# Turning the node coordinates of a two-layer graph network on VectorE and through DRAM instead of on TensorE, with the last pair's first graph handled early

## The chip, the core and the metric

The kernel runs on one core of a Trainium2 chip. The metric is device time in microseconds (us) of one execution, as a median of several. The core has five engines that each take their own instructions in written order: TensorE (PE in the profile, with its weight loads as PEld), VectorE (DVE), ScalarE (ACT), GpSimd (POOL) and SyncE (SP), which here issues nearly all DMAs. Matmul results land in PSUM, which has eight banks; everything else on the chip lies in SBUF, whose first dimension is the partition.

## The reference

There are 64 graphs of 256 nodes with 256 features, with a dense 0/1 adjacency each, all in float32. Layer 0 has a convolution branch (a 1x1 and a 17-tap convolution over nodes, both with batch norm), a message branch and a gated unit. Layer 1 is a graph convolution between two layer norms. Cut to what matters:

```python
s = x @ w_se.T + b_se                              # 3 coordinates for each node
sq = jnp.sum(s * s, axis=-1)
dist = sq[:, :, None] + sq[:, None, :] - 2.0 * jnp.einsum('bnd,bmd->bnm', s, s)
A = jnp.exp(-dist) * mask                          # mask is the adjacency
msg = jax.nn.relu(x @ w_msg.T + b_msg)
x_nmp = jnp.einsum('bnm,bmd->bnd', A, msg)
x_in = jnp.concatenate([x_conv, x_nmp], axis=-1)   # gates r, z, n from x_in and x
x = _layernorm(x + (1.0 - z) * nn_ + z * x)
...
h = layer_norm(x, ln_gamma, ln_beta)
agg = jnp.einsum('bij,bjh->bih', adj, h)
conv = jnp.einsum('bkh,ho->bko', agg, W_rel) + b_rel + jnp.einsum('bkh,ho->bko', h, W_root)
x = _layernorm(x + x + jax.nn.relu(conv))
```

The change touches the way that s gets from "nodes on partitions" to "coordinates on partitions", and the order of layer 1 for the last two graphs.

## The kernel before, in words

Graphs go in 32 pairs (function `pair(p)`), and the convolution goes in 8 batches of 8 graphs (`conv1`, `conv`); the first batch has its own setting-up of the filters. A pair takes these steps. Its x, turned so that features lie on partitions, is loaded (xT, L1077), and its adjacency (adjm, L1080). PE multiplies it by the message weights and, in three more columns, by the coordinate weights (ps_msg, L1095); DVE adds the bias (L1102).

**The coordinates.** ACT copies the three coordinates of each node into sts (L1104), POOL works out the squared lengths (L1109 to L1113) and puts -sq/2 beside them (L1112). PE turns this with two transposes (ps_sT, L1119). ACT copies the result twice into lr (L1120, with one row set to one by means of the small table `lone`, and L1121). Eight matmuls of four rows each (in the trace; four in the code) then give s.s - sq/2 for each pair of nodes (ps_dist, L1128). Each graph and node half has its own four partitions of lr, at 0, 32, 64 and 96. ACT takes the exponential (AT, L1132), DVE multiplies by the adjacency (L1135), and PE multiplies with the messages (ps_nmp, L1142).

**The gates.** 126 matmuls per pair (L1194), by a scheme of seven products in place of eight, or 144 by the plain way (L1180) in the first two pairs and the last. ACT and DVE make r, z, n and the sum x + layer 0 out of them: wT (L1285; in the last pair `turn_in`, L1218 to L1227, does it for one feature half of one graph at a time).

**Layer 1.** `norm` turns wT to nodes on partitions. Most pairs do that with one VectorE transpose in 32x32 blocks (L1302), four stores to DRAM (wd, L1306) and four loads (x1, L1310); the last pair does it with PE transposes (ps_wT, L1324). Statistics follow, with a power on POOL (L1344). `project` multiplies by both weight matrices (ps_hy, L1359), and DVE scales and adds on the way out (L1361). `aggregate` multiplies by the adjacency (ps_agg, L1373); then come DVE (L1376, L1377), the second norm and the store of the output (L1403). For the last pair (`apart`), norm and project run for graph 0 and then for graph 1; then aggregation for graph 0, and `last_nodes` (L1405), which aggregates, norms and stores graph 1 in two halves of its nodes. There is one copy of wT, x1 and HY, so pair p + 1 writes them when pair p has read them.

**The order of the work.** Nothing runs as it stands in the code. Each operation carries a key (`prog.at(key, step)`), most of them relative to `due = FIRST_GATES + p * PERIOD`. A planner (`scheduled`, L319) then walks through time: on each engine it takes, of the operations that are ready in its own estimate, the one with the smallest key, less a lead for DVE operations and for those that empty a PSUM bank. Its estimates of durations stand at L288 to L311. A load on SP is not planned before its key. The order that comes out is each engine's written program; at run time an instruction waits for its semaphores, and all behind it on its engine wait too. Operations in `prog.group()` stay together. `hold` and `need` add dependences: an instruction with `hold=[v]` goes after all earlier readers of v.

Of the kernel before, what the change touches and what calls it, by code (L numbers as in the profile page):

```python
# [14 lines left out]
F32 = mybir.dt.float32  # L15
# [3 lines left out]
P = 128  # L19
B, N, D = 64, 256, 256  # L20
C = D // P
# [33 lines left out]
OB = 7  # L55
HQ = 2 * M * C * (M + 1)
XC_SLOTS = BG + 2
FIRST_GATES, PERIOD, GATE_TIME = 124.4, 57.9, 16.7
AHEAD_FROM, AHEAD_TO, W_DEEP = -57.8, -17.6, 2
CONV1_FROM, CONV1_TO, CONV_FROM, CONV_OUT, CONV_TO = -10.0, 196.6, -12.4, -57.1, -31.9  # L60
PAIR_LEAD, FILTER_LEAD, LOAD_AHEAD = 31.8, 15.0, 22.3
SMALL_RUNS, TURN_FROM = 1.3, 2
KEEP = 7.7
LATE_LAG = 17.7
W_FROM, W_LAG = 2, 20.1
PLAIN, SUMS_FROM = (0, 1, B // 2 - 1), 2


# [190 lines left out]
def dram_cells(ap):  # L259

    name = ap.tensor.name
    if not name.startswith(("w2m", "xt", "hd", "wd")):
        return []
    dims = list(ap.ap)
    top = ap.offset + sum(s * (n - 1) for s, n in dims)
    return [(name, u) for u in range(ap.offset // DRAM_UNIT, top // DRAM_UNIT + 1)]


class Engine:
# [4 lines left out]
    def __getattr__(self, method):  # L274
        program, name = self.program, self.name

        def call(*args, hold=(), need=(), lines_up=0, **named):
            line = sys._getframe(1 + lines_up).f_lineno
            outs = [v for v in (named.get("out"), named.get("accum_out"), named.get("out_")) if v is not None]
            outs += [] if "out" in named else [args[0]]  # L280
            ins = [v for v in list(args) + list(named.values()) if not any(v is o for o in outs)]
            if method == "matmul" and not named.get("start", True):
                ins.append(outs[0])

            def places(vs):
                return [v if isinstance(v, View) else dram_cells(v) for v in vs
                        if isinstance(v, View) or hasattr(v, "tensor")]
            n = max((v.size() for v in outs if isinstance(v, View)), default=0)  # L288
            moved = 0
            if method == "dma_start":  # L290
                v = outs[0] if isinstance(outs[0], View) else named["in_"]
                dur, moved = 0.06, v.size() * v.at.shape[0] * 4
                if not isinstance(outs[0], View) and outs[0].tensor.name.startswith("w2m"):
                    moved *= 0.65
                if program.joined is not None:
                    moved *= SMALL_RUNS
            elif name == "tensor":
# [120 lines left out]
def gnn_two_layers(  # L418
# [65 lines left out]
    h_dram = tc.dram_tile([B // 2, 5, P, D], F32, name="hd")  # L484
    xt_dram = tc.dram_tile([B // 2, P, C, 2 * N], F32, name="xt")
    w_dram = tc.dram_tile([2, SQ, 2 * C * C, P // SQ, P], F32, name="wd")
    W2 = sb("w2all", [P, C, NM, D], "first")
    taps = sb("taps", [TAPS * OB, NM * OB], "filters")

# [455 lines left out]
    bms = sb("bms", [P, D + 4])  # L945
    wrr = sb("wrr", [P, C, 2 * D])
    hrow = sb("hrow", [P, 2 * D])
    lone = sb("lone", [LR, 2])
    gb = sb("gb", [P, 2, C])
    bih = sb("bih", [P, 3, C])  # L950
    bhh = sb("bhh", [P, 3, C])
    half_r = sb("half_r", [P, C])
    half_z = sb("half_z", [P, C])
    sts = sb("sts", [P, LR + P + 4])
    sts.base.fine = 0
    lr = sb("lr", [P, 2, N])
    prog.at(22.0, 0.001)
    ab = np.zeros((LR, 2), np.float32)
    for r in range(0, LR, SR):
        ab[r:r + 3, 0] = 1.0  # L960
        ab[r + 3, 1] = 1.0
    SP.dma_start(out=lone, in_=nc.inline_tensor(ab, name="last_row_one").ap())
    G.memset(sts, 0.0)
    V.memset(wms[:, :, D + 3:], 0.0)
    SP.dma_start(out=wms[:, :, :D], in_=wmsgT.rearrange("(c p) n -> p c n", p=P))
    SP.dma_start(out=wms[:, :, D:D + 3], in_=wseT.rearrange("(c p) n -> p c n", p=P))
# [105 lines left out]
    def pair(p):  # L1072
# [7 lines left out]
            SP.dma_start(out=adjm[:, g], in_=adjT[2 * p + g].rearrange("(c p) n -> p c n", p=P))  # L1080

        prog.at(due - 62, 0.6)
        at = p % 2 * 4
        st = sts[:, at:at + C * LR].rearrange("p (m e) -> p m e", m=C)

        def places(m):
            o = at + m * LR
            return sts[:, o:o + 4 * SR].rearrange("p (g r e) -> p g r e", g=2, r=2)[:, :, :, 0:3]
        idle = p < 2
        for g in range(2):  # L1090
            for m in range(C):
# [9 lines left out]
                    continue  # L1101
                V.tensor_add(msg[:, g, m], ps[:, :D + 4], bms)  # L1102
        for m in range(C):
            A.copy(places(m), msg[:, :, m, D:D + 3].unsqueeze(2).to_broadcast([P, 2, 2, 3]))  # L1104
        for g in range(2):
            A.activation(msg[:, g, :, :D], msg[:, g, :, :D], AF.Relu)
        sq, ns = next(sqs), next(nss)
        s = st[:, :, :3 * SR].rearrange("p m (r e) -> p m r e", e=SR)[:, :, ::2, 0:3]
# [3 lines left out]
        G.tensor_scalar(st[:, :, 3::SR].rearrange("p m (g r) -> p m g r", g=2), ns.unsqueeze(3).to_broadcast([P, C, 2, 2]), -0.5, None, ALU.mult)  # L1112
        G.tensor_scalar(ns, ns, -1.0, None, ALU.mult)  # L1113

        prog.at(due - 45, 0.3)
        ps = bank("ps_sT")
        with prog.group():
            for m in range(C):
                PE.transpose(ps[:LR, m * P:(m + 1) * P], st[:, m, :LR], ident, hold=[lr])  # L1119
        A.activation(lr[:LR, 0, :], ps[:LR, :N], AF.Identity, bias=lone[:, 1:2], scale=lone[:, 0:1])  # L1120
        A.copy(lr[:LR, 1, :], ps[:LR, :N])  # L1121
        prog.at(due - 38, 0.3)
        pss = [bank("ps_dist") for _ in range(2 * C)]
        with prog.group():
# [167 lines left out]
            return [(g, m, 2 * g + m) for g in gs for m in range(C)]  # L1292

        def norm(gs):
            prog.at(due + 2 * GATE_TIME + (4 if 0 in gs else -10), 0.3)
            q, sh = next(qs), next(shs)
            js = slice(2 * gs[0], 2 * gs[-1] + 2)
            total, squares, mv = next(totals), next(totals), next(mvs)
# [18 lines left out]
                        A.activation(HY[:, g, m, :D], x1[:, g, m, :], AF.Copy, accum_out=total[:, j:j + 1])  # L1317
            for g in gs if apart or p < W_FROM else ():
                ps = bank("ps_wT")
                with prog.group():  # L1320
                    for m in range(C):
                        for f in range(C):
                            at = m * D + f * P
                            PE.transpose(ps[:, at:at + P], wT[:, 2 * f + g, m * P:(m + 1) * P], ident,  # L1324
                                         hold=[x1[:, g]])
# [25 lines left out]
            return q  # L1351

        def project(gs, q):
            prog.at(due + 2 * GATE_TIME + (8 if 0 in gs else -6) + (0.0 if apart or p < W_FROM else LATE_LAG if late else W_LAG), 0.6)
            for g, m, j in spots(gs):
                ps = bank("ps_hy")
                with prog.group():
                    for f in range(C):
                        PE.matmul(ps, wT[:, 2 * f + g, m * P:(m + 1) * P], wrr[:, f, :], start=(f == 0),  # L1359
                                  stop=(f == C - 1), hold=[HY[:, g, m]], need=[] if apart else [q[:, 1, j:j + 1]])  # L1360
# [189 lines left out]
```

## Time and profile before

| what | value |
|---|---|
| median of 3 runs (lowest, highest) | 2005.71 us (2005.5, 2005.9) |
| the profiled execution: time, span | 2005.27 us, 2003.5 us |
| mean granted TensorE clock | 0.999 |
| PE busy | 1989.3 us, 99% |
| DVE, ACT, POOL busy | 1716.0, 1031.9, 286.2 us |
| DMA queue q1, share of 16 engines' span | 48.2% |
| ps_sT, 64 matmuls | 12.3 us busy |
| ps_dist, 256 matmuls | 22.8 us busy |

The span runs from the first instruction of the program to the end of the last. Busy time counts an engine's own work; matmuls are pipelined, so that the busy time of one group holds parts that overlap with its neighbours. The chain of waits goes back from the last instruction to what released each step, and so says which engine the end was waiting for at each moment.

### The profile page before, as it was taken

The page shows a single profiled execution, that of the slowest core. Times are in us where ns is not written, and L with a number is a line of the kernel's source. Part 1 is how long each engine was busy: PE and PEld are TensorE (multiplying, and loading weights), DVE is VectorE, ACT ScalarE, POOL GpSimd, SP SyncE. Part 2 cuts the span into 40 slices and gives each one's busy share as a digit, 9 for nine tenths or more (in the row PEclk, how much of TensorE's full clock was granted, in tenths as well). Part 3 has the DMA queues.
Part 4 walks back from the last instruction along what each step waited for, and adds up shares of the span by engine and source line. Part 5 has one row for each costly group of instructions (what it writes and reads, how often), then busy time and mean ns, then how long its engine had stood idle before and what let it go on. Part 6 is the DMA issues. An engine that isn't in the chain of part 4 may idle for free.

```text
span 2003.5 us, 28397 instructions
## 1 busy us (share of the span) xinstructions
PE 1989.3 (99%) x10068; PEld 1615.5 (81%) x10068; DVE 1716.0 (86%) x2632; ACT 1031.9 (52%) x2410; POOL 286.2 (14%) x521
## 2 busy tenths in 40 slices
PE   9999999999999999999999999999999999999997
PEld 6787888778888888778887788878888888887785
DVE  7787899999989998999979999899998999876755
ACT  7535433754456454655357545375535644556442
POOL 4200210111110111111011111011111111211001
PEclk9999999999999999999999999999999999999999
DMA  8844355535645456535645357453575245422311
GB/s 219 294 139 146 100 181 148 150 85 167 177 128 150 121 149 169 142 94 141 186 143 149 77 144 200 127 149 93 152 191 152 78 115 143 116 59 78 86 46 40
DMA packets 449114, 271.60 MB, mean 136 GB/s; under 512 B 247253, under 2 KB 433612, under 8 KB 448972
## 3 DMA queue, kind: packets, MB, share of 16 engines
q1 hardware_dynamic: 448430, 269.36, 48.2%
q8 instruction: 79, 1.29, 0.3%
q14 instruction: 63, 0.52, 0.1%
q10 hardware_dynamic: 542, 0.43, 0.1%
HBM read 193.05 MB, written 76.68 MB: 135 GB/s over the span
## 4 chain that ended last, share of the span: by engine, by line
PE 97%; DVE 1%; ACT 1%; POOL 0%; DMA 0%; issue 0%; POOLq 0%; ACTq 0%; DVEq 0%
PE ps_a L1194 22%; PE ps_k L716 17%; PE ps_d L1194 11%; PE ps_hy L1359 11%; PE ps_msg L1095 6%; PE ps_c L847 6%; PE ps_agg L1373 5%; PE ps_b L1194 5%; PE ps_nmp L1142 5%; PE ps_g L1180 4%; PE ps_w L574 2%; PE ps_dist L1128 1%; PE ps_tT L557 0%; PE ps_sT L1119 0%; PE ps_xTc L826 0%; PE ps_msg L1098 0%
## 5 line engine op out<-in xcount | busy, mean ns | idle before, releaser
L716 PEld LDWEIGHTS ps_k<-XF,cs 128*128 128x128 f32 x2632 | 312.6, 192 | 13.5 <-issue 7.0
L716 PE MATMUL ps_k<-XF,cs 128*128 128x128 f32 x2632 | 314.6, 275 | 0.0
L1359 PE MATMUL ps_hy<-wrr,wT 128*128 128x512 f32 x512 | 225.4, 592 | 0.0
L1194 PE MATMUL ps_a<-nmp,WB 128*128 128x256 f32 x696 | 207.1, 379 | 0.3 <-ACT nmp L1144 0.3
L1208 ACT ACTIVATE RG<-ps_a,bhh 128x512 f32<-128x512 f32 x116 | 79.4, 684 | 225.5 <-PE ps_a L1194 189.6
L1359 PEld LDWEIGHTS ps_hy<-wrr,wT 128*128 128x128 f32 x512 | 96.3, 190 | 107.7 <-issue 103.2
L1194 PE MATMUL ps_a<-tx,WB 128*128 128x256 f32 x522 | 155.7, 382 | 0.9 <-ACT RG L1208 0.9
L1194 PEld LDWEIGHTS ps_a<-nmp,WB 128*128 128x128 f32 x696 | 132.1, 190 | 18.7 <-ACT nmp L1144 0.7
L1095 PE MATMUL ps_msg<-wms,xT 128*128 128x260 f32 x512 | 133.2, 383 | 0.0
L688 DVE TENSOR_TENSOR XF<-XF 128x512 f32<-128x512 f32 (+3 forms) x128 | 126.8, 1007 | 4.9 <-ACT XF L769 3.1
L1142 PE MATMUL ps_nmp<-AT,msg 128*128 128x256 f32 x512 | 118.5, 379 | 0.0
L1361 DVE SCALAR_TENSOR_TENSOR HY<-ps_hy,q,hrow 128x512 f32<-128x512 f32 x128 | 95.2, 746 | 27.0 <-PE ps_hy L1359 21.9
L1373 PE MATMUL ps_agg<-HY,adja 128*128 128x256 f32 x504 | 117.6, 379 | 0.0
L1194 PEld LDWEIGHTS ps_a<-tx,WB 128*128 128x128 f32 x522 | 96.1, 190 | 23.0 <-issue 9.2
L1373 PEld LDWEIGHTS ps_agg<-HY,adja 128*128 128x128 f32 x504 | 94.7, 190 | 22.5 <-issue 9.3
L1383 ACT ACTIVATE HY<-HY 128x256 f32<-128x256 f32 x112 | 46.1, 415 | 129.5 <-DVE HY L1377 129.5
L1206 ACT COPY ZN<-ps_a 128x512 f32<-128x512 f32 x116 | 67.5, 582 | 84.7 <-PE ps_a L1194 84.7
L1095 PEld LDWEIGHTS ps_msg<-wms,xT 128*128 128x128 f32 x512 | 94.6, 190 | 18.7 <-issue 7.2
L851 ACT ACTIVATE xn<-ps_c,bnsh,bnsc 128x256 f32<-128x256 f32 x112 | 58.5, 564 | 98.5 <-PE ps_c L847 94.6
L847 PE MATMUL ps_c<-xTc,w 128*128 128x512 f32 x232 | 108.5, 594 | 0.0
L1142 PEld LDWEIGHTS ps_nmp<-AT,msg 128*128 128x128 f32 x512 | 96.1, 190 | 12.4
L1194 PE MATMUL ps_d<-nmp,WB 128*128 128x256 f32 x348 | 103.6, 379 | 1.3 <-DVE nmp L1163 1.3
(224 smaller groups left out, 4413.1 us busy)
## 6 DMA issues: line engine op xcount, KB each, us to landing
cs<-w2m SPq DMA_DIRECT2D x105, 768.0 KB, 5.0
adjm<-in_adjT_dram SPq DMA_DIRECT2D x64, 256.0 KB, 3.4
xT<-xt SPq DMA_DIRECT2D x32, 512.0 KB, 3.7
adja<-in_adjT_dram SPq DMA_DIRECT2D x64, 256.0 KB, 2.8
out_dram<-HY SPq DMA_DIRECT2D x63, 256.0 KB, 2.2
hd<-xn SPq DMA_DIRECT2D x28, 544.0 KB, 3.0
XF<-hd SPq DMA_DIRECT2D x28, 544.0 KB, 4.0
xt<-xTc SPq DMA_DIRECT2D x29, 512.0 KB, 3.6
```

What stands on the lines that cost most here:

```text
L688: (V.tensor_add if add else V.tensor_sub)(sl(o, n), sl(a, n), sl(b, n))
L716: PE.matmul(ps[:, o * P:(o + 1) * P], w(m, c)[:, o * P:(o + 1) * P], X[:, slot, c * P:(c + 1) * P], start=first and o == 0 and c == 0, sto ...
L847: PE.matmul(ps, w1[:, c, o * P:(o + 1) * P], xTc[:, c, :], start=(c == 0), stop=(c == C - 1), hold=[h[:, :, o]])
L1095: PE.matmul(ps[:, :D + 4], xT[:, c, g, m * P:(m + 1) * P], wms[:, c, :], start=(c == 0), stop=(c == C - 1 and not idle), hold=[msg[:, g, m]])
L1142: PE.matmul(ps[:, d * N:(d + 1) * N], msg[:, g, m, d * P:(d + 1) * P], AT[:, g, m, :], start=(m == 0), stop=(m == C - 1), hold=[nmp[:, :, g]])
L1180: PE.matmul(ps[:, h * N:(h + 1) * N], block[:, s, gate, :], right[s][2 * k + g], start=0 in ks and h == 0 and s == sources[0] and k == 0, ...
L1194: PE.matmul(ps[:, h * N:(h + 1) * N], block[:, s, gate, :], right[s][at], start=start and h == 0 and j == 0, stop=j == len(sources) - 1, s ...
L1206: A.copy(o, ps)
L1208: A.activation(o, ps, AF.Identity, bias=bhh[:, 2, f:f + 1])
L1359: PE.matmul(ps, wT[:, 2 * f + g, m * P:(m + 1) * P], wrr[:, f, :], start=(f == 0), stop=(f == C - 1), hold=[HY[:, g, m]], need=[] if apart ...
L1361: stt(HY[:, g, m, :], ps, q[:, 1, j:j + 1], hrow)
L1373: PE.matmul(ps[:, n_ * D:(n_ + 1) * D], adja[:, g, m, n_ * P:(n_ + 1) * P], HY[:, g, m, :D], start=(m == 0), stop=(m == C - 1))
```

## The change

The coordinates are laid out in sts with 32 columns for each half of the nodes, of which 16 are used: for graph g and use w, four fields. Use 0 has the three coordinates and a constant one, which is written once; use 1 has the coordinates and -sq/2. VectorE turns 32x32 blocks of all 128 partitions into `turned`; four DMAs store 16 rows of each block to a DRAM tile sd, so that each field becomes one row of 256 nodes, and four DMAs load these rows into lr, four partitions each. The PSUM bank ps_sT, its two PE transposes and the two ACT copies go.

In the last pair, norm, project and aggregation of graph 0 get keys at due + 12 to due + 14, before the gates of graph 1 end. Its transposes of wT are grouped by feature half, and its projection goes by feature half for both node halves in two PSUM banks, with the evacuations behind.

All planning constants get new values, and the planner counts 0.45 us of SP for each DMA where it counted 0.06. FIRST_GATES, PERIOD and GATE_TIME set the keys of pairs and gates; W_LAG and LATE_LAG are the lag of projection and aggregation.

```diff
-FIRST_GATES, PERIOD, GATE_TIME = 124.4, 57.9, 16.7
-AHEAD_FROM, AHEAD_TO, W_DEEP = -57.8, -17.6, 2
-CONV1_FROM, CONV1_TO, CONV_FROM, CONV_OUT, CONV_TO = -10.0, 196.6, -12.4, -57.1, -31.9
-PAIR_LEAD, FILTER_LEAD, LOAD_AHEAD = 31.8, 15.0, 22.3
+FIRST_GATES, PERIOD, GATE_TIME = 115.5, 58.7, 14.1
+AHEAD_FROM, AHEAD_TO, W_DEEP = -49.7, -53.1, 2
+CONV1_FROM, CONV1_TO, CONV_FROM, CONV_OUT, CONV_TO = -29.4, 99.1, -10.5, -47.1, -26.3
+PAIR_LEAD, FILTER_LEAD, LOAD_AHEAD = 50.5, 7.3, 20.3
 SMALL_RUNS, TURN_FROM = 1.3, 2
-KEEP = 7.7
-LATE_LAG = 17.7
-W_FROM, W_LAG = 2, 20.1
+KEEP = 13.3
+LATE_LAG = 28.9
+W_FROM, W_LAG = 2, 42.0
+COORDS = 41.8
...
-                dur, moved = 0.06, v.size() * v.at.shape[0] * 4
+                dur, moved = 0.45, v.size() * v.at.shape[0] * 4
...
+    s_dram = tc.dram_tile([2, P, D], F32, name="sd")
...
-    sts = sb("sts", [P, LR + P + 4])
-    sts.base.fine = 0
+    sts = sb("sts", [P, 2, C, SQ])
+    turned = sb("turned", [P, C, SQ])
...
     G.memset(sts, 0.0)
+    G.memset(sts[:, :, :, 3:16:8], 1.0)
...
-        at = p % 2 * 4
-        st = sts[:, at:at + C * LR].rearrange("p (m e) -> p m e", m=C)
...
+        st = sts[:, p % 2]
+        fields = st[:, :, :16].rearrange("p m (g w d) -> p m g w d", g=2, w=2)
...
-            A.copy(places(m), msg[:, :, m, D:D + 3].unsqueeze(2).to_broadcast([P, 2, 2, 3]))
+            A.copy(fields[:, m, :, :, 0:3], msg[:, :, m, D:D + 3].unsqueeze(2).to_broadcast([P, 2, 2, 3]))
...
-        G.tensor_scalar(st[:, :, 3::SR].rearrange("p m (g r) -> p m g r", g=2), ns.unsqueeze(3).to_broadcast([P, C, 2, 2]), -0.5, None, ALU.mult)
+        G.tensor_scalar(fields[:, :, :, 1, 3], ns, -0.5, None, ALU.mult)
...
-        prog.at(due - 45, 0.3)
-        ps = bank("ps_sT")
+        prog.at(due - COORDS, 0.3)
+        V.transpose(turned.rearrange("p m e -> p (m e)"), st.rearrange("p m e -> p (m e)"))
+        placed = s_dram[p % 2].rearrange("q (f n) -> (q f) n", n=N)[:16]
         with prog.group():
+            for a in range(P // SQ):
+                SP.dma_start(out=placed.rearrange("f (m b i) -> f m b i", m=C, i=SQ)[:, :, a, :],
+                             in_=turned[a * SQ:a * SQ + 16])
+        for g in range(2):
             for m in range(C):
-                PE.transpose(ps[:LR, m * P:(m + 1) * P], st[:, m, :LR], ident, hold=[lr])
-        A.activation(lr[:LR, 0, :], ps[:LR, :N], AF.Identity, bias=lone[:, 1:2], scale=lone[:, 0:1])
-        A.copy(lr[:LR, 1, :], ps[:LR, :N])
+                r = (2 * g + m) * SR
+                SP.dma_start(out=lr[r:r + 4], in_=placed.rearrange("(g w d) n -> g d w n", g=2, w=2)[g])
...
         def norm(gs):
-            prog.at(due + 2 * GATE_TIME + (4 if 0 in gs else -10), 0.3)
+            prog.at(due + 2 * GATE_TIME + (4 if not apart else -10 if gs[0] else 12 - 2 * GATE_TIME), 0.3)
...
-                with prog.group():
-                    for m in range(C):
-                        for f in range(C):
+                for fs in ((0,), (1,)) if apart else ((0, 1),):
+                    with prog.group():
+                        for m, f in ((m, f) for m in range(C) for f in fs):
...
         def project(gs, q):
-            prog.at(due + 2 * GATE_TIME + (8 if 0 in gs else -6) + (0.0 if apart or p < W_FROM else LATE_LAG if late else W_LAG), 0.6)
+            prog.at(due + 2 * GATE_TIME + (8 if not apart else -6 if gs[0] else 13 - 2 * GATE_TIME) + (0.0 if apart or p < W_FROM else LATE_LAG if late else W_LAG), 0.6)
+            if apart:
+                pss = [bank("ps_hy") for _ in range(C)]
+                for f in range(C):
+                    with prog.group():
+                        for g, m, j in spots(gs):
+                            PE.matmul(pss[m], wT[:, 2 * f + g, m * P:(m + 1) * P], wrr[:, f, :], start=(f == 0),
+                                      stop=(f == C - 1), hold=[HY[:, g, m]])
+                for g, m, j in spots(gs):
+                    stt(HY[:, g, m, :], pss[m], q[:, 1, j:j + 1], hrow)
+                return
...
         def aggregate(gs):
-            prog.at(due + 2 * GATE_TIME + 16 + (0.0 if apart or p < W_FROM else LATE_LAG if late else W_LAG), 0.4)
+            prog.at(due + 2 * GATE_TIME + (16 if not apart else 14 - 2 * GATE_TIME) + (0.0 if apart or p < W_FROM else LATE_LAG if late else W_LAG), 0.4)
```

More of the change, by code (lines that the diff above doesn't have):

```diff
@@ L261, in dram_cells @@
     name = ap.tensor.name
-    if not name.startswith(("w2m", "xt", "hd", "wd")):
+    if not name.startswith(("w2m", "xt", "hd", "wd", "sd")):
         return []
@@ L947, in gnn_two_layers @@
     hrow = sb("hrow", [P, 2 * D])
-    lone = sb("lone", [LR, 2])
     gb = sb("gb", [P, 2, C])
@@ L953, in gnn_two_layers @@
     half_z = sb("half_z", [P, C])
-    sts = sb("sts", [P, LR + P + 4])
-    sts.base.fine = 0
+    sts = sb("sts", [P, 2, C, SQ])
+    turned = sb("turned", [P, C, SQ])
     lr = sb("lr", [P, 2, N])
     prog.at(22.0, 0.001)
[L958 to L962, printed above, removed]
     G.memset(sts, 0.0)
+    G.memset(sts[:, :, :, 3:16:8], 1.0)
     V.memset(wms[:, :, D + 3:], 0.0)
@@ L1082, in pair @@
         prog.at(due - 62, 0.6)
-        at = p % 2 * 4
-        st = sts[:, at:at + C * LR].rearrange("p (m e) -> p m e", m=C)
-        def places(m):
-            o = at + m * LR
-            return sts[:, o:o + 4 * SR].rearrange("p (g r e) -> p g r e", g=2, r=2)[:, :, :, 0:3]
+        st = sts[:, p % 2]
+        fields = st[:, :, :16].rearrange("p m (g w d) -> p m g w d", g=2, w=2)
         idle = p < 2
@@ L1107, in pair @@
         sq, ns = next(sqs), next(nss)
-        s = st[:, :, :3 * SR].rearrange("p m (r e) -> p m r e", e=SR)[:, :, ::2, 0:3]
+        s = fields[:, :, :, 0, 0:3]
         G.tensor_mul(sq, s, s)
@@ L1359, in project @@
                         PE.matmul(ps, wT[:, 2 * f + g, m * P:(m + 1) * P], wrr[:, f, :], start=(f == 0),
-                                  stop=(f == C - 1), hold=[HY[:, g, m]], need=[] if apart else [q[:, 1, j:j + 1]])
+                                  stop=(f == C - 1), hold=[HY[:, g, m]], need=[q[:, 1, j:j + 1]])
                 stt(HY[:, g, m, :], ps, q[:, 1, j:j + 1], hrow)
         def aggregate(gs):
-            prog.at(due + 2 * GATE_TIME + 16 + (0.0 if apart or p < W_FROM else LATE_LAG if late else W_LAG), 0.4)
+            prog.at(due + 2 * GATE_TIME + (16 if not apart else 14 - 2 * GATE_TIME) + (0.0 if apart or p < W_FROM else LATE_LAG if late else W_LAG), 0.4)
             q, sh = next(q3s), next(shs)
```

## The prediction

> **What bounds the kernel.** I read the page first: busy time and chain of waits, then PE by stretches.
>
> ```profile
> PE 1989.3 (99%) x10068; PEld 1615.5 (81%) x10068; DVE 1716.0 (86%) x2632; ACT 1031.9 (52%) x2410; POOL 286.2 (14%) x521
> ...
> PE 97%; DVE 1%; ACT 1%; POOL 0%; DMA 0%; issue 0%; POOLq 0%; ACTq 0%; DVEq 0%
> ```
>
> PE is busy and on the ending chain nearly everywhere, with a granted clock of 1.00 in every stretch up to the tail. Busy time alone could hide gaps, so I checked the distance from one matmul's start to the next: each shape holds its own step (0.11 us for 128 columns, 0.216 for 256, 0.43 for 512). Outside the tail only five steps are over 0.4 us longer than that: about 0.4 at the start, 0.43 at 436 us, 0.45 at 1584, 0.76 at 1809 and 1.5 at 1898. So PE sets the time, and a PE instruction removed is worth its step. What PE does not set is the tail: the chain leaves PE at 1991.7 and the span ends at 2003.5. The profiled execution took 2005.27 us, 1.8 around its span of 2003.5; the median of the runs shown is 0.44 above it, so I add my sum to 2005.71.
>
> **Step 1: the transposes of the coordinates go from PE.** From the chain of waits near the end (start, length, what):
>
> ```profile
> 1879.15 3.45 PE ps_agg L1373 x16
> 1882.61 0.22 PE ps_sT L1119 x2
> 1882.83 2.16 PE ps_a L1194 x10
> ```
>
> PE goes from aggregation through two transposes to the next pair's gates without a break, and two cost 0.22 us. There are 64, all with the same 0.109 us step: 64 x 0.109 = **7.0 us off PE**. The tile's view (shortest, median and longest in ns) says something longer:
>
> ```profile
> L1119 PE MATMUL ps_sT<-ident,sts x64: 272/273/317, 99.2 to 1925.5; 128*100 128x128 f32 x64
> L1120 ACT ACTIVATE lr<-ps_sT,lone x32: 546/563/567, 99.6 to 1925.8; 100x256 f32<-100x256 f32 x32
> L1121 ACT COPY lr<-ps_sT x32: 352/361/369, 100.1 to 1926.3; 100x256 f32<-100x256 f32 x32
> ```
>
> 273 ns is one transpose from start to end, and its end overlaps the next matmul; I take the step. The Trainium skill ("TensorE: Matmul & The Clock Gate", Part 4: PE-mode transpose) gives about 275 ns inside a kernel, and the row agrees as a duration; taken as PE time per transpose it would make the gain 64 x 0.275 = 17.6 us (an estimate from that page). Rival D is that case, from the row. The two ACT copies also go (0.56 + 0.36 = 0.92 us per pair, 29.6 in all), worth nothing: ACT is busy half the time and nothing on PE waits long for it. The matmuls of ps_dist keep their four rows and 256 columns, so they cost the same.
>
> **Step 2: what replaces them.** DVE gets one 32x32 transpose of 64 columns per pair. The 1024-column one (L1302) takes 1.25 us and a 4-column operation 0.16, so by a line between them 0.16 + 60 x 1.07 ns = 0.22 us, 7 in all. The steady stage has room for it:
>
> ```profile
> 1200.00:1600.00 400.00, 399.71 (x2034) 327.92 (x2033) 359.94 (x539) 212.73 (x507) 52.17 (x101) 1.00 0.53 144
> ```
>
> After the stretch and its length come the busy times of PE, PEld, DVE, ACT, POOL. DVE is idle for 40 of 400 us, and seven pairs add 1.5. I cost it at nothing; uncovered it is 7 us. SP gets eight DMAs per pair, four 4 KB stores to sd and four 8 KB loads into lr, and waits between them for the stores to land. No row has such sizes. The nearest:
>
> ```profile
> wd<-HY SPq DMA_DIRECT2D x116, 128.0 KB, 3.5
> x<-wd SPq DMA_DIRECT2D x116, 128.0 KB, 3.1
> xn<-in_x_dram SPq DMA_DIRECT2D x192, 64.0 KB, 2.4
> ```
>
> (Queue, count, size, median us to landing.) One issue takes SP 0.49 us (the xn loads) to 0.67 (the wd stores). Short end, by the fastest landings: 0.22 on DVE, stores 3 x 0.49 + 2.4, loads the same: 8.0 us. The same route with 512 KB, last pair but one: DVE's transpose ends at 1945.8, the loads start at 1951.4, DVE has x1 at 1956.2, so 10.5 us. Long end, by the slowest landing of these transfers, 7.7 us: 0.2 + 2 x (3 x 0.67 + 7.7) = 19.6. I take 10. The Trainium skill ("DMA: Bandwidth & Descriptors", Anatomy of one DMA) has a fixed part of about 2.0 us per DMA, fitted on another issue path, and by that the chain would be 0.2 + 2 x (1.5 + 2.0) = 7.2 us; the rows of this trace are longer.
>
> This is paid only if ps_dist, its one reader, stands at PE's head before it lands: PE takes instructions in the written order, so gates and convolution products would queue behind it. The distance now, in a middle pair:
>
> ```profile
> 1004.09 0.56 POOL L1112 TENSOR_SCALAR sts<-ns 128x8 f32<-128x8 f32 x1
> ...
> 1029.35 0.71 PE L1128 MATMUL ps_dist<-lr 4*128 4x256 f32 x8
> ```
>
> 24.7 us from finished coordinates to ps_dist. Read so for all 32 pairs, it is 14.6 to 24.7 us in 17, 10.1 to 13.3 in 12, and 6.8, 7.5 and 8.7 in pairs 0, 1 and 27. The position comes from keys (coordinates at due - 62, ps_dist at due - 38, both unchanged), with gates and another pair's projection between. The new PERIOD and GATE_TIME place more of the gates there (from due - 58.7 on, with 20.7 of their 28.2 units before -38; now 19.9 of 33.4), W_LAG moves a projection to about due - 39, and aggregation out. That is much the same cover. A 10 us chain costs 3.2 + 2.5 + 1.3 = 7.0 if those three pairs keep their distances, 0 if the planner, which knows part of the latency, gives them other PE work. I take **+0.7**, near the covered end, since 29 of 32 rows are covered. SP's waiting also holds the loads queued behind, the two-deep filter loads (cs) above all: 8 issues of about 0.6 and 3 us of waiting, 8 us per pair. The wd route does the same to them now (SP waited there 54.2 us in 54 waits) and no ps_k matmul waits for a DMA in the profile; I add nothing. If that cover failed, it would be rival C.
>
> **Step 3: the last pair.** The end of the chain now:
>
> ```profile
> 1973.60 8.63 PE ps_g L1180 x40
> 1982.24 0.44 PE ps_wT L1324 x4
> 1982.67 3.44 PE ps_hy L1359 x8
> 1986.11 0.44 PE ps_wT L1324 x4
> 1986.55 3.44 PE ps_hy L1359 x8
> 1989.98 1.74 PE ps_agg L1373 x8
> ```
>
> The last gates end at 1982.24; the first graph's layer 1 (0.44 + 3.44 + 1.74 = 5.62 us) then covers DVE and ACT while they finish the second graph. The change puts these 5.62 us among the second graph's gates, so the gates end 5.6 later and the rest stands bare. By this timeline's rows, from the gates' end: wT after 2.7 (L1222 to L1227 end at 1984.98), transposes 3.1, statistics to evacuated HY another 4.2 (1987.07 to 1991.25) = 7.3, aggregation 1.0, then DVE from L1415 without the first graph's statistics and q 3.3, POOL, sh and ACT 1.6, DMA to span end 2.5: 15.7. With the 5.6 that makes 21.3, and today 2003.5 - 1982.24 = 21.3. I count **0**: PE is taken off the chain and latency takes its place. Bounds: -2 if DVE interleaves better, +3 if the first graph's work still sits on DVE then; it must also wait for pair 30's readers of wT, HY and x1, since the diff has no second copy of these, only two PSUM banks held together. The split transposes and f-order of the projection are inside these terms.
>
> The bare chain leaves PE idle from about 4.0 (projection done) to 7.3 us after the gates, 3.3 us. The trace shows how long PE may idle:
>
> ```profile
> 1996.00:1998.00 2.00, 0.00 (x0) 0.00 (x0) 1.75 (x9) 0.03 (x1) 0.67 (x2) 1.00 0.00 0
> 1998.00:2000.00 2.00, 0.00 (x0) 0.00 (x0) 0.32 (x2) 1.78 (x4) 1.10 (x2) 0.64 0.19 66
> ```
>
> (The third number from the right is the granted clock.) The last matmul ends at 1993.4 and the clock is still full up to 1998, so 3.3 us should pass. The Trainium skill ("TensorE: Matmul & The Clock Gate", Part 1) says one idle window of about 3.4 us halves the clock, a rule that speaks against the change; then the last 1.74 us of aggregation would take 3.5, some 1.7 more. It is within the +3.
>
> **Keys.** The other edited constants reorder a program without PE gaps, at the same amount of work. I take the existing 3.5 us of gaps as unchanged; gone or doubled, -3.5 to +3.5.
>
> **Sum.** 2005.7 - 7.0 + 0.7 + 0 = **1999.4 us**.
>
> **Rivals.** A, the forecast: below 2001.7, chance 0.66. B, the gain is mostly eaten: three or more pairs wait for lr in full (+7.0), or the tail's +3 meets new gaps, 2002 to 2008. For it: the three short distances and the bare tail. Against it: the order is made anew around longer DMAs. Chance 0.21. C, slower: the DMA chain is long, near 13.5 us (landings of 4.7 us, as several wd stores have), and PE waits at ps_dist in many pairs. With today's distances, what is missing is 6.7, 6.0 and 4.8 in the three, and 0.2 to 3.4 in the twelve, about 40 us: 2039. It decides from 11 us of waiting in all, 0.35 per pair (7.0 of gain plus 4.0). For it: eight dependent DMAs where ACT needed 0.9 us. Against it: PE's order is keyed well behind the coordinates. Chance 0.11. D, a transpose is worth its whole 273 ns: 2005.7 - 17.5 = 1988; the even step beside it speaks against it. Chance 0.02.
>
> Within 0.2% (4.0 us, about what this measurement can tell from no change) is B; faster is A and D, 0.68; slower is C, 0.11. The low end is the forecast with the tail's -2 and the gaps gone: 1994. The high end takes in B: 2008.
>
> **What would show it.** Right: no ps_sT on PE, PE busy lower by about 7, no ps_dist wait on DMA, a PE gap of 3 to 4 us before the last aggregation, the span's end 21 us after today's place of the gates less 7. Wrong: PE waiting at ps_dist for lr, ps_k waiting for cs, or ps_agg of the first graph behind the last gates. What would make it wrong most easily is the DMA chain in the short pairs, at the start, where the stores of w2m (10.9 to 11.7 us to landing) share the queues.

## The result, and the profile after

The changed kernel takes 1997.68 us (median of six runs, 1996.39 to 1998.19) where the kernel before takes 2005.72 (2005.1 to 2005.9): a ratio of 0.9959, 95% interval 0.9947 to 0.9972, so 8.0 us faster. The forecast was 1999.4. The profiled execution of the changed kernel took 1997.69 us, with a span of 1995.9; against the span of before that is 7.6 us less.

From the page of the kernel after, the busy times and the chain of waits by engine:

```profile
PE 1983.0 (99%) x10004; PEld 1609.8 (81%) x10004; DVE 1714.5 (86%) x2664; ACT 1014.0 (51%) x2346; POOL 282.2 (14%) x522
...
PE 98%; DVE 1%; DMA 1%; issue 0%; ACT 0%; POOL 0%; SPq 0%; POOLq 0%; ACTq 0%; DVEq 0%
```

PE has 64 instructions fewer and 6.3 us less busy time, and it still sets the time. The view of the tile sd, with the shortest, median and longest issue in ns:

```profile
L1113 SPq DMA_DIRECT2D sd<-turned x128: 547/592/657, 102.5 to 1918.6; - x128
L1118 SPq DMA_DIRECT2D lr<-sd x128: 254/298/446, 106.4 to 1922.6; - x128
```

A store holds SP for 0.59 us, a load for 0.30 us. DVE's transpose into `turned` (L1109) takes 0.245 us. The waits of PE (what waited, for what; us in total, times, longest):

```profile
PE ps_agg L1419 <- ACT x L1347: 2.0, 1, 2.0
PE ps_a L1191 <- ACT ZN L1203: 1.9, 2, 1.3
```

The others are 1.1 us and less. No matmul of ps_dist waits for lr, and none of ps_k for a filter load. From POOL's last write of the coordinates to ps_dist there are now 11.3 us at the least (pair 31), and up to 37.7.

The chain of waits at the end, by start and length in us:

```profile
1966.75 4.32 PE ps_g L1177 x20
1971.06 0.22 PE ps_wT L1321 x2
1971.28 4.32 PE ps_g L1177 x20
1975.60 0.44 PE ps_wT L1321 x4
1976.04 3.44 PE ps_hy L1357 x8
...
1979.69 1.72 PE ps_hy L1357 x4
1981.41 1.74 PE ps_agg L1380 x8
...
1986.90 1.32 PE ps_agg L1419 x4
```

The last gates end at 1975.60, 6.64 us earlier than before. Of the first graph only two transposes (0.22 us, at 1971.06) stand among the second's gates. Its other transposes, its projection (1976.04) and its aggregation (1981.41) stand behind them. From the gates' end to the span's end it is 20.3 us, where it was 21.3.

The 7.6 us of the spans add up from this: 64 steps of 0.109 are 7.0; the two transposes that moved ahead take 0.2 back, new gaps about another 0.2; the tail gives 1.0. These are two single executions. The kernel after and its variants with the old last pair, with own buffers and with the second graph first have the same order on PE up to the last pair, and still their executions stand up to 0.8 us apart at 87 us, so parts under 1 us are no firmer than that.

Two of the prediction's own signs went the wrong way: the first graph's aggregation stands behind the last gates, and PE's wait before the last aggregation is 2.0 us, not 3 to 4.

### The profile page after: what moved, and what is told of

It reads as the page before. It is cut to its first block, busy times and chain, and to the rows that moved or that the text cites. A ratio compares the mean times of both kernels' runs of the same rounds, so it can differ in the third digit from the quotient of the medians.

```text
span 1995.9 us, 28498 instructions
## 1 busy us (share of the span) xinstructions
PE 1983.0 (99%) x10004; PEld 1609.8 (81%) x10004; DVE 1714.5 (86%) x2664; ACT 1014.0 (51%) x2346; POOL 282.2 (14%) x522
## 4 chain that ended last, share of the span: by engine, by line
PE 98%; DVE 1%; DMA 1%; issue 0%; ACT 0%; POOL 0%; SPq 0%; POOLq 0%; ACTq 0%; DVEq 0%
PE ps_a L1191 22%; PE ps_k L718 16%; PE ps_d L1191 11%; PE ps_hy L1366 11%; PE ps_msg L1088 6%; PE ps_nmp L1139 6%; PE ps_c L849 6%; PE ps_b L1191 6%; PE ps_agg L1380 5%; PE ps_g L1177 5%; PE ps_w L576 2%; PE ps_dist L1125 1%; PE ps_tT L559 0%; PE ps_xTc L828 0%; DMA w2m<-w2all 0%
## 5 line engine op out<-in xcount | busy, mean ns | idle before, releaser
L1366 PEld LDWEIGHTS ps_hy<-wrr,wT 128*128 128x128 f32 x496 | 92.3, 190 | 87.9 <-issue 81.9
L1191 PE MATMUL ps_a<-xc,WB 128*128 128x256 f32 x348 | 103.5, 379 | 0.0
L1191 PE MATMUL ps_a<-tc,WB 128*128 128x256 f32 x348 | 103.5, 379 | 0.0
```

The lines of the kernel that those rows point to most:

```text
L1191: PE.matmul(ps[:, h * N:(h + 1) * N], block[:, s, gate, :], right[s][at], start=start and h == 0 and j == 0, stop=j == len(sources) - 1, s ...
```

## The experiments

Where a text on record names its theories by a letter, S is the forecast's reasoning (each part is worth its PE steps, and the rest stays covered). Its rivals are O (the new constants, with the order that they make, carry the gain), C (the late DMA chain of rival C) and D (a transpose is worth its whole duration). "Lost" is, here and below, the sum over PE's matmuls of the distance to the next matmul's start, less that shape's usual step, up to the last gates. It was 13.0 us before and is 13.3 after; some 0.2 us per pair of this stand at the edges of ps_dist in both.

### The coordinates alone

The kernel before with the new route, and none of the other edits.

```diff
 W_FROM, W_LAG = 2, 20.1
+COORDS = 41.8
...
-        ps = bank("ps_sT")
+        V.transpose(turned.rearrange("p m e -> p (m e)"), st.rearrange("p m e -> p (m e)"))
+        placed = s_dram[p % 2].rearrange("q (f n) -> (q f) n", n=N)[:16]
```

> The kernel before with the coordinates' part of the change alone: VectorE transpose, four stores and four loads per pair; all planning constants, the planner's DMA cost and the last pair as before. Theory S (PE's steps): 64 transposes of 0.109 us go, so 7.0 us less, 1998.7 us, give or take 1.5 for the new order. Rival O (the gain comes from the re-planned order): about 2005. Rival C (the DMA chain is late): ps_dist waits for lr and the time is above 2005. Rival D (a transpose is worth 0.273 us): 1988.

Measured: 2017.86 us (2015.06 to 2020.82), ratio 1.0062 [1.005, 1.0075]. This is 12.2 us **slower** than before, and no theory had it. The waits of PE:

```profile
PE ps_d L1191 <- DVE nmp L1160: 7.9, 5, 2.6
PE ps_a L1191 <- ACT ZN L1203: 3.0, 5, 0.7
```

None, down to the shortest, is for lr or for a DMA of the route, so it isn't C. The longest is of the gates for a DVE operation. The timeline of DVE in front of it (start, length, operation):

```profile
1113.29 1.23 DVE L1282 SCALAR_TENSOR_TENSOR wT<-ZN,RG 128x1024 f32<-128x1024 f32 x1
1114.55 1.25 DVE L1299 STREAM_TRANSPOSE HY<-wT 128x1024 f32<-128x1024 f32 x1
1115.71 0.65 DVE L1160 TENSOR_TENSOR nmp<-nmp 128x512 f32<-128x512 f32 x1
```

L1160 makes the difference of the message result that the seven-product gates need. The last operations of the previous pair's gates, and that pair's transpose, now stand ahead of it on DVE: it starts 6.2 us after the message matmuls (ps_nmp) of its pair end, where in the kernel before the same pair's first difference started 0.9 us after them. PE is empty for 2.6 us until 1116.4. Then its clock is halved, as the stretches show (the third number from the right is the granted clock):

```profile
1114.00:1116.00 2.00, 0.00 (x0) 0.00 (x0) 1.97 (x3) 0.69 (x1) 0.00 (x0) 1.00 0.88 223
1118.00:1120.00 2.00, 2.00 (x6) 1.52 (x6) 2.00 (x2) 0.88 (x1) 0.00 (x0) 0.50 1.05 178
```

Lost is 32.2 us, 19.2 more than before: the 7.0 of the transposes and the 12.2 of the loss together. The planner, told of a longer chain, has made another order, with PE's and DVE's work at other distances.

### The last pair alone

The kernel before with the three edits to norm, project and aggregate.

```diff
-            prog.at(due + 2 * GATE_TIME + (4 if 0 in gs else -10), 0.3)
+            prog.at(due + 2 * GATE_TIME + (4 if not apart else -10 if gs[0] else 12 - 2 * GATE_TIME), 0.3)
```

> The kernel before with the last pair's part alone (keys of graph 0, transposes grouped by feature half, projection by feature half). Theory S, as the trace after shows the tail: about 1.0 us less, 2004.7. Step 3 of the prediction: 0, 2005.7. If the first graph's layer 1 really goes ahead of the last gates with the old lags, the gates end up to 5.6 us later and what follows is shorter by as much.

Measured: 2005.13 us (2004.66 to 2005.72), ratio 0.9997 [0.9989, 1.0006]: no difference that can be told. In the profiled execution PE waits 2.05 us before the last aggregation, as in the kernel after (2.04), but here the clock is halved behind the wait. The eight matmuls of that aggregation take 3.65 us where they took 2.17 there, and from their start to the end of the span it is 9.8 us where it was 9.0. That is most of the tail's 1.0.

### The constants alone

All the new planning constants and the 0.45 us per DMA, with the old coordinates and the old last pair.

```diff
-FIRST_GATES, PERIOD, GATE_TIME = 124.4, 57.9, 16.7
+FIRST_GATES, PERIOD, GATE_TIME = 115.5, 58.7, 14.1
...
-                dur, moved = 0.06, v.size() * v.at.shape[0] * 4
+                dur, moved = 0.45, v.size() * v.at.shape[0] * 4
```

> The kernel before with the new planning constants and the planner's 0.45 us per DMA alone; coordinates and last pair as before. Theory S: PE has the same steps to do and nearly no gaps to lose, so 2005.7, give or take 3. Rival O: about 1998, most of the gain.

Measured: 2013.14 us (2011.99 to 2015.16), ratio 1.0039 [1.0026, 1.0053], 7.5 us slower. Its longest wait on PE is one that the changed kernel can't have:

```profile
PE ps_sT L1120 <- POOL sts L1113: 3.1, 1, 3.1
```

PE's transposes of the coordinates come 3.1 us too early, at 148 us; behind that gap the clock is 0.5 for 6.8 us. This place holds 7.85 of the lost 19.8 us. So the constants aren't a gain by themselves: the order that they make doesn't suit the old route, as the old constants don't suit the new one.

### After, with the old last pair

```diff
-            prog.at(due + 2 * GATE_TIME + (4 if not apart else -10 if gs[0] else 12 - 2 * GATE_TIME), 0.3)
+            prog.at(due + 2 * GATE_TIME + (4 if 0 in gs else -10), 0.3)
```

(and the other two edits undone in the same way)

> The changed kernel with the last pair's part undone: graph 0 and graph 1 of the last pair keyed, grouped and projected as before. Theory S: what the tail gained is lost, about 1.0 us more than the changed kernel, 1998.7. If the last pair's part brought nothing: 1997.7.

Measured: 1997.79 us (1997.36 to 1998.35), ratio 0.9961 [0.9948, 0.9973]. By the medians the last pair's edits are worth 0.1 us, which is nothing. In the profiled execution the tail is 21.3 us again, as before, but the gates end at 1974.71, 0.9 sooner than in the kernel after. Of this, 0.2 are the two transposes that stay behind the gates, and 0.7 had built up ahead of the last pair between two executions of the same order. So a tail shorter by 1.0, less 0.2, may be real and hidden in executions that spread over 1 to 1.8 us; the medians don't show it. The gain of 8 us is that of the coordinates and the constants together.

### Two spare transposes per pair

The kernel after, with two more transposes of 100 columns (of constant data, into the bank of ps_dist before ps_dist writes it) just ahead of each pair's ps_dist: what was taken off PE, put back without its waits.

```diff
+            spare = op.calls[0][2][0].base.real
+            for m in range(C):
+                one_line(op.calls[0][4])(nc.tensor.transpose, [spare[:LR, m * P:(m + 1) * P], ones.made()[:, :LR], ident.made()], {})
```

> The changed kernel, in its own order, with two more PE transposes per pair just ahead of ps_dist, into the bank that ps_dist then overwrites; nothing reads them. Theory S: 64 x 0.109 = 7.0 us more, 2004.7. Rival D: 64 x 0.273 = 17.5 more, 2015.2. If PE had slack there: 1997.7.

Measured: 2004.6 us (2003.23 to 2004.71), ratio 0.9993 [0.9984, 1.0002]: 6.9 us above the kernel after, 0.108 per transpose. The traces say the same more closely. PE has the same order in both, and from 100 to 1866 us it falls behind by 0.22 us at each place with two spare transposes, which is 6.5 us for 60 transposes, and by less than 0.1 us in all elsewhere. The step is the price, and D falls. (The total is less exact than that: in the first 100 us this execution gained 0.6 us on the other, and in the tail it lost 0.6, where the clock is halved here and isn't in the kernel after.)

### One and three round trips more

The kernel after, where the stored coordinates are copied to a second DRAM tile and back, once or three times, before they are loaded.

```diff
+            for _ in range(1):
+                nc.sync.dma_start(out=there, in_=here)
+                nc.sync.dma_start(out=here, in_=there)
```

> The changed kernel, in its own order, with the stored coordinates copied to a second DRAM tile and back once before the loads: two more DMAs in series, some 5.6 us longer (2 x (0.6 issue + 2.2 landing)). In the trace after, ps_dist starts 2.3 us after the last load's issue in the last pair, 5.5 in pairs 22 and 29, 6 and more in the others; with 2 us for the landing, the cover theory gives a wait of about 5 us in the last pair, 2 in pair 29 and next to none elsewhere: 6 to 7 us more, 2004. If every pair had stood near its limit: 32 x 5.6, 2177. If the filter loads behind it on SP came late, the PE waits would stand at ps_k and not at ps_dist.

Measured: 2020.65 us (2016.46 to 2024.24), ratio 1.0075 [1.0062, 1.0087], 23 us above the kernel after. The waits of PE:

```profile
PE ps_a L1192 <- ACT ZN L1204: 6.7, 3, 5.0
PE ps_k L719 <- DMA cs<-w2m: 6.2, 5, 3.3
PE ps_dist L1126 <- DMA lr<-sd: 2.5, 3, 1.2
```

The reader of the longer chain, ps_dist, waits only 2.5 us in three pairs: the cover is nearly as wide as this chain. The rest comes over SP. It waits for the copies in its written order, and the filter loads behind it come late (6.2 us). After three of the stalls (at 473.6, 1613.7 and 1948.2) the clock is 0.5 for 6.8 us, which costs 3.4 us each time. Those 10.2 us, with 2.5, 6.2 and the 4.8 by which the wait for ZN grew, are 23.7 of the 26.5 us between the two profiled executions (this one is the slowest of its five). The sum that was expected counted the reader and left out SP's queue and the clock.

> The same with three round trips, some 17 us longer. The cover theory: most pairs have 4 to 9 us of cover beyond the landing, so about 24 pairs wait some 8 to 12 us each, at ps_dist: 2180 to 2290 us. Where the four loads are spread out today by other waits on SP (pairs 0, 1, 6, 10, 14, 18, 22), the longer chain fits in and nothing waits. If SP's queue is what gives way, PE waits at ps_k for filters as well.

Measured, in one run: 2277.94 us, with a mean granted clock of 0.944. The waits of PE:

```profile
PE ps_dist L1126 <- DMA lr<-sd: 87.0, 24, 8.8
```

Here ps_dist waits 24 times, for 87 us, and the filter loads cost another 52.0. This is rival C's mechanism: it exists, and it decides at a longer chain than the change has. The time lies in the expected range, but not by the expected account: 24 waits of 8 to 12 us were to make it, and they are 3.6 us on average. All of PE's waits come to about 190 of the 280 us that the span grew by; the rest stands beside the lower clock and wasn't taken apart.

### Buffers of its own for the last pair

The kernel after, with second copies of wT, x1, HY and the adjacency for the last pair, laid in a part of the convolution's data that is no longer needed, so that nothing there waits for pair 30's readers.

```diff
-            pair(p)
+            if p == B // 2 - 1:
+                pair(p, X[:, 20:24], X[:, 8:12].rearrange("p (g c) e -> p g c e", g=2),
...
+            else:
+                pair(p, wT, x1, HY, adja)
```

> The changed kernel with a second copy of wT, x1, HY and adja for the last pair, in the convolution's area, which is free by then; so its first graph need not wait for the readers of pair 30. In the written order, the first graph's transposes and projection then stand before the last gates. Step 3 of the prediction: 3.9 us of PE work leave the end and as much bare latency takes their place, so the changed kernel's time, 1997.7, give or take 1. Rival: the end is shorter by what left it, 1994.

Measured: 2001.05 us (2000.74 to 2001.62), ratio 0.9977 [0.9968, 0.9987], 3.4 us above the kernel after. The order did change: the first graph's transposes and projection are ahead of the last gates. The chain from there:

```profile
1969.80 8.63 PE ps_g L1177 x40
1978.43 1.74 PE ps_agg L1380 x8
...
1980.19 0.70 DVE XF L1383
...
1980.99 0.69 DVE XF L1384
1981.68 0.34 DVE RG L1222
```

and the stretch in which PE takes up work again:

```profile
1988.00:1990.00 2.00, 1.02 (x3) 0.79 (x4) 1.50 (x3) 1.36 (x3) 0.05 (x1) 0.50 0.34 116
```

The gates end at 1978.43, later by the work put ahead of them, and the tail from there is 20.7 us, no shorter. Aggregation of the first graph still follows the gates, and its two DVE operations (L1383, L1384, 1.4 us) stand ahead of the second graph's turning (L1222). PE is then empty for 3.84 us before the last aggregation. The clock falls to 0.50, and those matmuls take 3.78 us where full clock would give 1.89: more than half of the 3.4 us that were lost.

### The coordinates in the old order

The kernel before, with every operation on PE, DVE, ACT and POOL in its old order, the transposes and the two ACT copies left out, and the new route (DVE's transpose, four stores, four loads) issued directly behind POOL's last write.

```diff
-                PE.transpose(ps[:LR, m * P:(m + 1) * P], st[:, m, :LR], ident, hold=[lr])
+                prog.add("tensor", lambda: None, (), {}, 0, [st], [ps, lr], 0.109)
...
+        if op in placed_after:
+            nc.vector.transpose(turned.made().rearrange("p m e -> p (m e)"), sts.made()[:, p % 2].rearrange("p m e -> p (m e)"))
```

> The kernel before with every instruction in the order that it had; only the 64 PE transposes and the 64 ACT copies are left out, and VectorE's transpose, the stores and the loads stand right behind POOL's last write of a pair. The planner sees none of it. Theory S with the planner's order to blame for the loss of the coordinates alone: 7.0 us less, and a few us of waits at ps_dist in pairs 0 and 1, whose 6.8 and 7.5 us are shorter than the fastest chain seen, under 8.7: 1999 to 2002. Rival P (the route itself, by its work on VectorE and SP's queue, costs the 19 us that the coordinates alone lost): 2018.

Measured: 2009.43 us (2007.69 to 2011.37), ratio 1.0019 [1.001, 1.0029], 3.8 us slower than before, with 25.0 us lost; it lies between the two theories, and neither had it. Two places hold 11.4 of the 12 that are too many: 6.45 at 157 us and 4.96 at 249. The waits of PE there:

```profile
PE ps_k L717 <- DMA cs<-w2m: 3.2, 1, 3.2
PE ps_dist L1127 <- DMA lr<-sd: 2.0, 1, 2.0
```

In pair 1, the last of the four stores, issued at 151.99, took 6.0 us to land, in a stage that is dense with the convolution's loads and stores; the loads went out at 158.1 and ps_dist started at 159.75. At 249 us a filter load is late. After both the clock is 0.5, for 6.8 and 3.4 us. From there on nothing is lost. The stretch from 262 to 1900 us, PE's busy time after the length, first in this kernel:

```profile
262.00:1900.00 1638.00, 1636.82 (x8299) 1342.65 (x8292) 1459.46 (x2233) 837.93 (x2002) 221.16 (x429) 1.00 0.49 136
```

and in the kernel before:

```profile
262.00:1900.00 1638.00, 1635.48 (x8296) 1338.63 (x8295) 1451.48 (x2198) 856.04 (x2050) 226.46 (x429) 1.00 0.49 134
```

PE is idle for 1.2 us of 1638 there, and for 2.5 before. In 30 of 32 pairs the old order covers the route, at distances of 8.8 to 24.5 us. Pair 0 has only 6.5 us, and loses 0.3 among its ps_dist matmuls. So the loss of the coordinates alone isn't the route's latency in the pairs: it is the new order that the planner makes for it.

### The planner's price of a DMA

First the coordinates alone, with 0.45 us of SP per DMA in the planner; then the kernel after with the old last pair and the old price of 0.06.

```diff
-                dur, moved = 0.06, v.size() * v.at.shape[0] * 4
+                dur, moved = 0.45, v.size() * v.at.shape[0] * 4
```

> The coordinates' part alone, as in the first experiment, with the planner's 0.45 us per DMA and all keys as before. If the loss came from a planner that thinks SP's issues are free: near 1999. If it came from keys that leave ps_dist, the mask and the differences of nmp no time before the gates: 2010 to 2020, as without it.

Measured: 2016.22 us (2015.53 to 2017.62), ratio 1.0055 [1.0042, 1.0067]: 1.6 us better than without, with 30.3 lost, and the executions of the two overlap. The price alone mends little.

> The coordinates' part with all the new keys and lags, the last pair as before, and the planner's DMA cost at the old 0.06 us. If the keys make the room: 1998 to 2000, as with 0.45. If the DMA cost is what counts: 2010 or more.

Measured: 2002.38 us (2000.13 to 2004.17), ratio 0.9985 [0.9976, 0.9994]. The new keys bring 15.5 us over the coordinates alone; the price brings another 4.6, down to the 1997.79 of the kernel after with the old last pair. Both theories missed: the keys are most of it, but not all. Where the 4.6 stand isn't shown, as the profiled execution is the fastest of its eleven (2000.13).

### The second graph first

The kernel after, with the first graph's aggregation keyed behind the second's projection.

```diff
-            prog.at(due + 2 * GATE_TIME + (16 if not apart else 14 - 2 * GATE_TIME) +
+            prog.at(due + 2 * GATE_TIME + (16 if not apart else -3) +
```

> The changed kernel with the last pair's aggregation of graph 0 keyed behind graph 1's projection, so that PE finishes that projection 1.7 us sooner and VectorE evacuates it ahead of graph 0's additions and statistics. In the trace after, the last aggregation starts at 1986.9, when VectorE has done 2.9 us of graph 0's work; by the timeline it could start near 1985.4: 1.5 us less, 1996.2, and PE's idle time of 2.0 us before it goes. If the end hangs on VectorE's total and not on its order: 1997.7.

Measured: 1996.49 us (1996.14 to 1997.04), ratio 0.9955 [0.9941, 0.9969]. The chain has the second graph's whole projection (3.44 us from 1979.59) ahead of that aggregation, and PE's 2.0 us wait in the tail is gone. It is the fastest of all by its median, 1.2 us below the kernel after; the two weren't run side by side and their intervals overlap.

## Why the prediction came out, step by step

The forecast of 1999.4 is 1.7 us too high: the 0.7 of step 2 wasn't paid, and the other 1.0 is of the size of the tail's gain and of the spread between executions.

**Step 1, 7.0 us: right.** The spare transposes measured 0.108 each, and D's price of 0.273 would have shown 17.5 us. The Trainium skill ("TensorE: Matmul & The Clock Gate", Part 4: PE-mode transpose) has some 275 ns; the run shows that this is a duration, and not what a transpose costs in a busy queue.

**Step 2, +0.7: covered, as forecast, with a chain that was taken too long.** No ps_dist waits, so the cost was 0. In one pair of the coordinates alone, ps_dist followed POOL's last write by 8.7 us without a wait, so the chain can be at most that, not 10. In the old order's pair 0 it is shorter still: ps_dist begins 6.5 us after that write and its matmuls are held up for 0.3 us, so some 7 us at most. The Trainium skill ("DMA: Bandwidth & Descriptors", Anatomy of one DMA) led to an estimate of 7.2, which is close to that. DVE's transpose was sized at 0.22 and takes 0.245. SP's waiting was costed at nothing: in the kernel after that holds, but with the old order, or with one round trip more, the filter loads came late for just this reason. The rule of thumb used there (the wd route does the same to them now) didn't show how little room was left.

**Step 3, 0: the sum held by luck, the mechanism failed.** It had the first graph's 5.62 us among the second's gates. 0.22 us went there. What the step named as a condition, pair 30's readers of x1, wT and HY, is what the own buffers took away; the projection then did move, and the time got worse. The tail from the gates' end should then have been 15.7 us and was 20.7: the first graph's aggregation and its work on DVE were still there, as the step's +3 had it, and the clock fell. Its claim that a bare gap of 3.3 us should pass without a drop of the clock isn't safe: 3.84 us halved it here, 2.6 in the coordinates alone, and 2.05 in the last pair alone, though 2.93 passed in the run with the keys and the old price. The row it rested on (full clock for 4.6 us after the last matmul of before) shows one gap at one place, and the place decides, as the last section works out. So it is luck, too, that the kernel after kept its full clock behind the 2.0 us in the profiled execution. The Trainium skill ("TensorE: Matmul & The Clock Gate", Part 1) has the clock halved after one idle window of about 3.4 us. In the drops listed there, 2.0 to 3.0 us of a step of 3.41 us were empty and not the whole, and the measurement decides.

**Keys, 0 with 3.5 either way: the term that was mis-sized.** In the sum it stands right, with 13.0 lost before and 13.3 after. As a property of the constants it is wrong: they cost 7.5 us without the new route, and the new route costs 12.2 without them. "The same amount of work" was true and didn't decide. The cover that step 2 counted on is made by these constants, and step 2 and this term were priced as if they were independent.

**The rivals.** B's and C's mechanisms both exist in variants (stalls of a few us at the start and in the tail; ps_dist late in 24 pairs), not in this kernel. That the 7.0 are nearly the whole of the gain follows from the steps; the tail's 1.0 stands in the bookkeeping of two executions, and the medians with and without the last pair's edits don't bear it out. Which of the single keys makes the order good was not tried, and stays open; so does whether the later place of ps_dist alone puts the message difference behind DVE's gate work in the coordinates alone, which was read from the order and not tried by itself.

## What to carry to other kernels

An instruction taken off a full engine is worth its step, but only if what replaces it stays covered; with an order planned by keys, a new latency and new keys are one edit, and either of them tested alone can show a loss. Ask of a longer DMA chain not only whether its reader waits, but what stands behind it on the queue that waits for it. Before work is moved ahead to fill a gap elsewhere, count the gap that it leaves: from some 2 us on, an empty PE can cost the gap and half a clock after it.

## What the runs showed of the hardware

A PE gap can be paid again behind it, and its length alone doesn't decide. Within an execution the half clock begins on a fixed grid. With one round trip more it begins at 473.63, 1613.68, 1948.19 and 2013.04 us, which are 334, 98 and 19 steps of 3.413 us apart, and every stretch of it that ends before the tail is 3.41, 6.83, 10.24 or 13.65 us long. What counts is how much of one such step PE is empty:

| run | PE's gap, us | ends at | most of it in one step | clock behind it |
|---|---|---|---|---|
| coordinates alone | 2.61 | 1116.42 | 2.61 | 0.5 |
| constants alone | 3.07 | 150.92 | 2.99 | 0.5 |
| coordinates in the old order | 3.16 | 252.78 | 3.04 | 0.5 |
| own buffers | 3.84 | 1988.98 | 2.78 | 0.5 |
| last pair alone | 2.05 | 1994.16 | 2.05 | 0.5 |
| coordinates in the old order | 2.04 | 159.75 | 2.04 | 0.5 |
| coordinates alone, DMA price | 1.99 | 635.61 | 1.99 | 0.5 |
| coordinates and keys, old price | 2.93 | 1824.75 | 1.94 | 1.00 |
| coordinates alone | 2.01 | 637.53 | 1.84 | 1.00 |
| kernel after | 2.04 | 1986.90 | 1.24 | 1.00 |

The same gap of 2.0 us before the last aggregation shows it. (PE's busy time stands first after the length of a stretch, the clock third from the right.) In the last pair alone the gap lies in one step, and the next step runs at half clock:

```profile
1990.85:1994.26 3.41, 1.36 (x4) 0.33 (x4) 3.16 (x10) 0.77 (x2) 0.70 (x1) 1.00 0.00 0
1994.26:1997.68 3.42, 3.42 (x8) 2.24 (x8) 1.88 (x6) 1.35 (x3) 0.00 (x0) 0.50 0.21 75
```

In the kernel after an edge of the grid cuts it in two:

```profile
1982.27:1985.69 3.42, 2.58 (x9) 1.17 (x7) 2.30 (x6) 0.00 (x0) 0.53 (x1) 1.00 0.00 0
1985.69:1989.10 3.41, 2.17 (x8) 1.35 (x8) 2.54 (x8) 2.11 (x4) 0.70 (x1) 1.00 0.00 0
1989.10:1992.51 3.41, 0.00 (x0) 0.00 (x0) 2.50 (x11) 0.60 (x1) 1.10 (x2) 1.00 0.23 79
```

Over all runs, every full-clock step with more than 2.0 us empty was followed by half clock. With 1.99 to 2.00 both were seen. Of the steps with less, three were, with 1.4 to 1.7 us empty, and these hold matmuls of ps_dist with waits between them. The grid lies differently in each of the profiled executions, so the same kernel may meet the drop in one execution and not in another; no kernel was profiled twice to show it. A half clock of 6.8 us under a busy PE costs 3.4 us.

A small DMA's price depends on when it is issued. In most pairs of the old order the first load, which waits for the stores, goes out 1.2 to 1.3 us after SP is done with the last store, so 1.8 to 1.9 after that store's issue began; in the dense stage at 152 us it went out 5.5 us after, and the store took 6.0 us from its issue to land.
